# Two 32-key attention stages put in written order, with the norms in quarters and a standing diagonal bank for the causal values

## The chip, the cores and the metric

The kernel runs on one core of one Trainium2 chip. The metric is the device time of one execution in microseconds, as the median of several runs. All data is fp32.

## What is computed

`x` is 64 batches of 32 rows of 256; `ctx_512` is 64 batches of 257 keys of 64. Six blocks follow one another, each adding to `x`:

```python
x = x + L0_xattn(layernorm(x), ctx_512)   # stage A: causal, 16 heads of 16, keys from the context; only its first 32 matter
x = x + L0_attn(layernorm(x))             # stage B: 16 heads of 128, one shared key and value
x = x + L0_ffn(layernorm(x))              # stage C: 4 of 16 blocks chosen per row
x = x + L1_xattn(layernorm(x), ctx_512)   # stage D: 257 rotated keys
x = x + L1_attn(layernorm(x))             # stage E: causal, 16 query heads of 16, 4 key and value groups
x = x + L1_ffn(layernorm(x))              # stage F: one of 8 experts per row
```

The change touches A and E, the two attentions with 32 keys:

```python
# A: no biases; q = x Wq, k, v = ctx Wkv
# E: grouped, with biases
q  = einsum('bse,hed->bhsd', x, Wq) + bq
kg = einsum('bse,ged->bgsd', x, Wk) + bk
vg = einsum('bse,ged->bgsd', x, Wv) + bv
k, v = repeat(kg, 4), repeat(vg, 4)          # over heads
scores = where(causal, einsum('bhqd,bhkd->bhqk', q, k) / sqrt(16), -inf)
out = einsum('bhqk,bhkd->bhqd', softmax(scores), v)
```

## The kernel before

The 2048 rows of `x` are 16 tiles of 128 partitions (`xs[t]`); a tile is four batches. Four tiles are a group (`g`), for which the norm, the transposition and the query and key products are done at once. A loop over tiles does the rest, one slot `t` of the loop working on tile `t + 1` (scores), `t` (the transposed probabilities), `t - 1` (the weighted values), and, in A, `t - 2` (the output product).

A tile's way is: `scores` multiplies queries with keys that stand in a two-wide masked form (`kd`), 32 small matmuls, into four banks of PSUM (tile `S`). `softmax_rows` evicts them with scale and causal mask on VectorE (DVE), takes the row maximum there, subtracts it on GpSimd (POOL), takes exp on ScalarE (ACT), sums on DVE and inverts. In A the division is done on POOL before the transposition, in E after the weighted sum. `heads_on_partitions` transposes the probabilities by TensorE (PE) and copies them out on ACT (`pT`). The values must stand on a block diagonal by head (`vd`), so that one matmul serves four heads: in A four DVE multiplications with the mask `m4` make it from PSUM, in E one DVE addition of the bias (`vb`) and four POOL multiplications. `gather` multiplies.

Layer norms are `ln_group`: statistics of four tiles (`stats`), the inverse root (`rstd_of`; with `power=True` on POOL, an addition and a power), the shift, and four outputs in the tag `xn`, which has four buffers. The normed tiles are transposed into `xT`.

In E, routing for stage F runs beside the attention: `route_stats` a slot after a tile is finished, then for groups of four `route_norm`, `route_turn`, `route` and `send` in successive slots. `send` computes the place of each row and starts one indirect DMA per tile from POOL's queue.

What sets the order: `tc.manual_schedule(engines={PE})` keeps PE in the order of the Python text in A and E; DVE, ACT and POOL are ordered by the planner of the tile framework there. In B all four engines follow the text, in C PE and ACT, in D and F PE. SyncE (SP) issues the plain DMAs in the planner's order everywhere. A scratch area `srt` is filled by SP with 1 MB DMAs, and 12 MB of expert weights (`fw`) load while E begins.

[...] Before, E has S (4), PT, o, and two for the tag "mm", which the transpositions, the query and key products, the value product and the routing products share.

Of the kernel before, what the change touches and what calls it, by code (L numbers as in the profile page):

```python
# [45 lines left out]
def perceiver_kernel(ctx: ExitStack, tc: tile.TileContext, a: dict, out: bass.AP):  # L46
# [107 lines left out]

    def ln_group(g, name, twice=False, act=False, power=False):

        mv = sm(f"lnm_{name}{g}", [P, 4, 2])
        for i in range(4):
            stats(mv[:, i, :], xs[4 * g + i], f"{name}{g}_{i}")
        rs = rstd_of(mv, 4, f"{name}{g}", power)  # L160
        if twice:

            v2 = sm(f"lnw_{name}{g}", [P, 4, 2])
            nc.vector.tensor_tensor(v2[:, :, 1], mv[:, :, 1], rs, ALU.mult)
            nc.vector.tensor_tensor(v2[:, :, 1], v2[:, :, 1], rs, ALU.mult)
            rs2 = rstd_of(v2, 4, f"{name}{g}b", power)
            nc.vector.tensor_tensor(rs2, rs2, rs, ALU.mult)
            rs = rs2
        sh = sm(f"lnh_{name}{g}", [P, 4])
        nc.vector.scalar_tensor_tensor(sh, mv[:, :, 0], -1.0, rs, ALU.mult, ALU.mult)  # L170
        xn = []
        for i in range(4):
            y = xnp.tile([P, D], F32, tag="xn", name=f"xn_{name}{g}_{i}")
            x_ = xs[4 * g + i]
            if act:
                nc.scalar.activation(
                    y, x_, AF.Identity, scale=rs[:, i : i + 1], bias=sh[:, i : i + 1]
                )
            else:
                nc.vector.scalar_tensor_tensor(  # L180
                    y,
                    x_,
                    rs[:, i : i + 1],
                    sh[:, i : i + 1].to_broadcast([P, D]),
                    ALU.mult,
                    ALU.add,
                )
            xn.append(y)
        return xn
# [22 lines left out]
    def softmax_rows(s_ps, t, work, name):  # L212


        s = work.tile([P, NH, S], F32, tag="s", name=f"s_{name}{t}")
        nc.vector.scalar_tensor_tensor(
            s.rearrange("p (r h) k -> p r (h k)", r=4),
            s_ps[:, :, :P],
            0.25,
            bc(caus4, 1, 4),  # L220
            ALU.mult,
            ALU.add,
        )
        mx = sm(f"mx_{name}{t}", [P, NH])
        nc.vector.tensor_reduce(mx, s, AX.X, ALU.max)
        nc.gpsimd.tensor_tensor(s, s, bc(mx, 2, S), ALU.subtract)
        nc.scalar.activation(s, s, AF.Exp)
        su = sm(f"su_{name}{t}", [P, NH])
        nc.vector.tensor_reduce(su, s, AX.X, ALU.add)
        ri = sm(f"ri_{name}{t}", [P, NH])  # L230
        nc.vector.reciprocal(ri, su)
        return s, ri
# [31 lines left out]
    def scores(ps, qT, kd, i, name):  # L264

        s_ps = ps.tile([P, 4, 512], F32, tag="S", name=f"S_{name}")
        for o in range(KC):
            for j in range(4):
                for r in range(4):
                    rs = slice(32 * r, 32 * r + 32)  # L270
                    nc.tensor.matmul(
                        s_ps[j * S : (j + 1) * S, r, o * 64 : (o + 1) * 64],
                        qT[rs, o, i * P + j * S : i * P + (j + 1) * S],
                        kd[rs, o, 4 * i + j].rearrange("p w k -> p (w k)"),
                        start=True,
                        stop=True,
                        tile_position=(32 * r, 32 * j),
                    )
        return s_ps
# [56 lines left out]
    with tc.tile_pool(name="wA", bufs=2) as work, tc.tile_pool(  # L336
# [3 lines left out]
    ) as ps2, tc.manual_schedule(engines={mybir.EngineType.PE}):  # L340
# [15 lines left out]
        def group(g, part):  # L356
# [7 lines left out]
            if part == 0:  # L364
                feats[g][2] = transposed(ln_group(g, "a", power=True), ps2, g, "a")
# [27 lines left out]
        def score(t):  # L393
            g, i = divmod(t, 4)
            qT, kd, _ = feats[g]
            s_ps = scores(ps1, qT, kd, i, f"a{t}")
            sc[t] = softmax_rows(s_ps, t, work, "a")
            s, ri = sc[t]
            nc.gpsimd.tensor_tensor(s, s, bc(ri, 2, S), ALU.mult)
# [56 lines left out]
        for _ in range(18):  # L456
            nc.tensor.matmul(warm, pad[:, 0:P], pad[:, 0:256], start=True, stop=True)
        for part in (0, 1, 2):
            group(0, part)
        score(0)  # L460
        values(0)

# [7 lines left out]
        for t in range(NT + 2):  # L470
# [8 lines left out]
            if t < NT:  # L479
                turned[t] = heads_on_partitions(sc.pop(t)[0], ps1, t, work, "a")  # L480
            if 1 <= t <= NT:
                gather(t - 1)
            group(t // 4 + 1, t % 4)
# [653 lines left out]
    with mbw, wd1:  # L1137
# [3 lines left out]
        with tc.tile_pool(name="wD", bufs=2) as work, tc.tile_pool(  # L1141
# [7 lines left out]

            def e_group_start(g):  # L1150
                feats[g] = (
                    e_w.tile([P, KC, 512], F32, tag="qT", name=f"qTe{g}"),
                    e_w.tile([P, KC, 16, 2, S], F32, tag="kd", name=f"kde{g}"),
# [3 lines left out]
            def e_features(g, part, o, ps):  # L1157

                qT, kd, xT = feats[g]
                q_ps = ps.tile([P, 512], F32, tag="mm", name=f"qe{g}_{o}_{part}")  # L1160
# [193 lines left out]
            steps[48] = lambda: lat.update(e=ln_group(0, "e", power=True))  # L1354
            steps[50] = lambda: e_group_start(0)
            steps[61] = lambda: lat.update(e1=ln_group(1, "e", power=True))
            for z, b_ in enumerate((51, 55, 56, 58, 59, 60)):
# [112 lines left out]
    with tc.tile_pool(name="wE", bufs=2) as work, tc.tile_pool(  # L1470
        name="psE", bufs=1, space=PSUM
    ) as ps1, tc.tile_pool(name="psE2", bufs=2, space=PSUM) as ps2, tc.manual_schedule(
        engines={mybir.EngineType.PE}
    ):
        sc, vals, turned = {}, {}, {}
        lat[1] = lat["e1"]

        def group(g, part):

            if g >= NG:  # L1480
                return
            if part == 0:
                e_group_start(g)
                for k in range(KC):
                    transposed_part(lat.pop(g) if k else lat[g], feats[g][2], ps2, k, f"e{g}")
            if part in (1, 2):
                for o in range(KC):
                    e_features(g, part, o, ps2)
            if part == 3 and g + 1 < NG:
                lat[g + 1] = ln_group(g + 1, "e", power=True)  # L1490

        def score(t):
            g, i = divmod(t, 4)
            qT, kd, xT = feats[g]
            s_ps = scores(ps1, qT, kd, i, f"e{t}")
            sc[t] = softmax_rows(s_ps, t, work, "e")
            v_ps = ps2.tile([P, 4, DC], F32, tag="mm", name=f"ve{t}")
            for j in range(4):
                for k in range(KC):
                    for r in range(4):  # L1500
                        nc.tensor.matmul(
                            v_ps[32 * r : 32 * r + 32, j, :],
                            xT[:, k, i * P + j * S : i * P + (j + 1) * S],
# [4 lines left out]
            vb = work.tile([P, 4, DC], F32, tag="vb", name=f"vbe{t}", bufs=1)  # L1508
            nc.vector.tensor_tensor(vb, v_ps, bc(vec[:, V_BV : V_BV + DC], 1, 4), ALU.add)
            vd = vals[t] = work.tile([P, 4, 4, 4, NH], F32, tag="vd", name=f"vde{t}", bufs=3)  # L1510
            for j in range(4):
                nc.gpsimd.tensor_tensor(
                    vd[:, j],
                    bc(vb[:, j, :].rearrange("p (g d) -> p g d", g=4), 2, 4),
                    bc(bc(m4, 2, 16), 1, 4),
                    ALU.mult,
                )

        def gather(t):
            pT, vd, ri = turned.pop(t), vals.pop(t), sc.pop(t)[1]  # L1520
            o_ps = ps1.tile([P, D], F32, tag="o", name=f"oe{t}")
            for c in range(4):
                for j in range(4):
                    nc.tensor.matmul(
                        o_ps[j * S : (j + 1) * S, c * 64 : (c + 1) * 64],
                        pT[:, c, j * S : (j + 1) * S],
                        vd[:, j, c].rearrange("p h d -> p (h d)"),
                        start=True,
                        stop=True,
                    )  # L1530
            on = work.tile([P, D], F32, tag="on", name=f"one{t}", bufs=1)
            nc.vector.tensor_tensor(
                on.rearrange("p (h d) -> p h d", h=NH),
                o_ps.rearrange("p (h d) -> p h d", h=NH),
                bc(ri, 2, 16),
                ALU.mult,
# [6 lines left out]
        def route_stats(t):  # L1543
            rows[t] = sm(f"lnm_f{t}", [P, 1, 2])
            stats(rows[t][:, 0, :], xs[t], f"f{t}")

        def route_norm(ts):
            n_ = len(ts)
            mv = sm(f"lnq_f{ts[0]}", [P, n_, 2])
            for i, t in enumerate(ts):  # L1550
                nc.gpsimd.tensor_copy(mv[:, i, :], rows[t][:, 0, :])
            rs = rstd_of(mv, n_, f"f{ts[0]}", True)
            sh = sm(f"lnh_f{ts[0]}", [P, n_])
            nc.vector.scalar_tensor_tensor(sh, mv[:, :, 0], -1.0, rs, ALU.mult, ALU.mult)
            rows[ts] = []
            for i, t in enumerate(ts):
                y = xnp.tile([P, D], F32, tag="xn", name=f"xn_f{t}")
                nc.scalar.activation(
                    y, xs[t], AF.Identity, scale=rs[:, i : i + 1], bias=sh[:, i : i + 1]
                )  # L1560
                rows[ts].append(y)
                nc.gpsimd.tensor_copy(xf[t][:, D + 2 : D + 3], rs[:, i : i + 1])
                nc.gpsimd.tensor_copy(xf[t][:, D + 3 : DP], sh[:, i : i + 1])
# [115 lines left out]

        score(0)  # L1680
        group(1, 0)
        group(1, 1)
        for t in range(NT + 1):


            if t + 1 < NT:
                score(t + 1)
            if t < NT:
                turned[t] = heads_on_partitions(sc[t][0], ps1, t, work, "e")
            if t > 1:  # L1690
                group(t // 4 + 1, t % 4)
            if t > 0:
                gather(t - 1)
                route_stats(t - 1)
            for step, ts in routing.get(t, ()):
                step(ts)
        for step, ts in routing[NT + 1]:
# [192 lines left out]
```

## Time and profile before

| | us |
|---|---|
| median of 3 runs | 1302.73 (1302.47 to 1304.62) |
| the profiled execution | 1298.15, of which its span 1296.4 |
| A: first scores to the last `ya` | 18.5 to 151.5 |
| B, C and D | 151.5 to 992.5 |
| E: first scores to the last `oe` | 992.5 to 1125.3 |
| routing's end, to the first row fetched | 1125.3 to 1146.9 |
| F | 1146.9 to 1296.4 |

The stages are cut by the timeline of PE. Busy time of PE is modelled and includes time at a lower clock, so a busy PE is not PE at its peak. A group's row names the line, the engine, the operation, output and input, count, busy time, mean time of one, and the idle time before it with what ended most of that. "issue" is a wait for nothing that the profile shows.

### The profile page before, as it was taken

What the parts mean: (1) busy time and instruction counts of PE and PEld (TensorE: products, weight loads), DVE (VectorE), ACT (ScalarE), POOL (GpSimd) and SP (SyncE); (2) the same over time, 40 slices, a digit from 0 to 9 for tenths busy, and PEclk for the clock granted to TensorE, in tenths of its full rate; (3) what the DMA queues carried; (4) which work ended last, traced back from release to release, by engine and by line L of the source; (5) the groups of instructions that cost most, each with busy time, mean ns of one, the idle gap of its engine ahead of it and who ended that gap; (6) DMA issues with size and microseconds to landing.
All of it is one profiled execution on the core that took longest, in us unless ns stands there. A gap on an engine that the chain in (4) does not pass through costs nothing. (4 is left out here: it accounts for less than half of the span.)

```text
span 1296.4 us, 26028 instructions
## 1 busy us (share of the span) xinstructions
PE 1187.8 (92%) x10189; PEld 833.3 (64%) x10189; DVE 769.0 (59%) x1751; ACT 540.1 (42%) x1255; POOL 389.7 (30%) x504
## 2 busy tenths in 40 slices
PE   6898999999999999999989999999998687669997
PEld 4555767767767566777756767777766455536664
DVE  5665345778758865533288877777674574334432
ACT  2336354554544641222365656556563233211111
POOL 2232251554524631000055252000002577621111
PEclk8889999999999989979999989999999788669999
DMA  7991110111021220912154353111103700011110
GB/s 232 309 332 36 28 42 1 41 42 41 25 83 42 59 65 2 283 33 68 44 149 131 62 143 93 46 35 48 34 1 127 266 3 19 22 50 42 43 39 18
DMA packets 94588, 103.10 MB, mean 80 GB/s; under 512 B 37664, under 2 KB 71201, under 8 KB 93986
## 3 DMA queue, kind: packets, MB, share of 16 engines
q1 hardware_dynamic: 92594, 97.19, 25.8%
q0 software_dynamic: 1872, 4.23, 0.9%
q8 instruction: 82, 1.34, 0.4%
q14 instruction: 40, 0.33, 0.1%
HBM read 69.45 MB, written 32.85 MB: 79 GB/s over the span
## 5 line engine op out<-in xcount | busy, mean ns | idle before, releaser
L1261 ACT ACTIVATE pp<-Sd,nm 128x257 f32<-128x257 f32 x256 | 118.2, 475 | 71.9 <-DVE nm L1257 66.1
L706 PE MATMUL qb<-xT_b,b_q 128*128 128x256 f32 x512 | 123.0, 389 | 0.0
L706 PEld LDWEIGHTS qb<-xT_b,b_q 128*128 128x128 f32 x512 | 95.6, 191 | 39.5 <-issue 19.6
L797 PE MATMUL yb<-b_o,oTb 128*128 128x256 f32 x512 | 116.1, 386 | 0.0
L797 PEld LDWEIGHTS yb<-b_o,oTb 128*128 128x128 f32 x512 | 98.4, 194 | 14.3 <-issue 1.0
L1270 DVE TENSOR_TENSOR pp<-pp,rd 128x514 f32<-128x514 f32 x128 | 98.4, 769 | 2.1
L1257 DVE TENSOR_REDUCE nm<-Sd 128x2 f32<-128x514 f32 x128 | 83.0, 685 | 19.2 <-PE Sd L1249 19.0
L1292 ACT COPY pTd<-pt 128x512 f32<-128x512 f32 x112 | 61.5, 599 | 52.1 <-PE pt L1286 52.1
L1309 PE MATMUL od<-pTd,na 128*64 128x256 f32 x480 | 66.3, 397 | 8.2 <-issue 6.5
L725 POOL TENSOR_TENSOR q2b<-qTb 128x512 f32<-128x512 f32 x64 | 65.2, 1048 | 27.0 <-ACT qTb L714 27.0
L1249 PE MATMUL Sd<-ct,qTd 64*128 64x257 f32 x480 | 69.2, 405 | 0.4 <-ACT pp L1261 0.2
L816 POOL TENSOR_TENSOR ynb<-ynb,vec 128x256 f32<-128x256 f32 x16 | 11.6, 726 | 191.3 <-DVE ynb L815 191.3
L714 ACT COPY qTb<-qb 128x512 f32<-128x512 f32 x64 | 37.5, 585 | 72.2 <-PE qb L706 70.6
L1286 PE MATMUL pt<-cst,pp 128*128 128x128 f32 x512 | 66.9, 274 | 0.0
L1286 PEld LDWEIGHTS pt<-cst,pp 128*128 128x128 f32 x512 | 59.0, 141 | 9.9 <-issue 5.6
L1068 PE MATMUL qd<-xT_d,d_m 128*128 128x256 f32 x256 | 64.4, 395 | 0.2 <-ACT xT_d L201 0.2
L759 DVE RECIPROCAL rqb<-rqb 128x512 f32<-128x512 f32 x16 | 53.5, 3344 | 17.8 <-ACT rqb L754 17.8
L588 PE MATMUL yc<-c,hc 128*128 128x256 f32 x256 | 59.4, 388 | 2.7 <-DVE hc L583 2.7
L1325 PE MATMUL yd<-d_n,co 128*128 128x256 f32 x256 | 61.5, 395 | 0.0
L1765 POOL DMA_INDIRECT out_dram<-os,ti x23 | 22.7, 986 | 124.4 <-DVE os L1762 100.8
L1068 PEld LDWEIGHTS qd<-xT_d,d_m 128*128 128x128 f32 x256 | 46.8, 192 | 17.0 <-issue 6.4
L773 DVE RECIPROCAL rdb<-denb 128x512 f32<-128x512 f32 x16 | 53.7, 3355 | 5.8 <-PE denb L771 5.6
(365 smaller groups left out, 2394.5 us busy)
## 6 DMA issues: line engine op xcount, KB each, us to landing
srt<-pad SPq DMA_DIRECT2D x17, 1040.0 KB
mb<-maskd SPq DMA_DIRECT2D x64, 128.0 KB
ct<-ctd SPq DMA_DIRECT2D x30, 257.0 KB
rct<-in_ctxT_dram SPq DMA_DIRECT2D x32, 128.5 KB
rrt<-in_ctxT_dram SPq DMA_DIRECT2D x64, 64.2 KB
ctd<-rct SPq DMA_DIRECT2D x32, 128.5 KB
nad<-rna SPq DMA_DIRECT2D x16, 256.0 KB
fw<-in_f_wg_dram SPq DMA_DIRECT2D x8, 512.0 KB
```

Source lines behind the costliest of these rows:

```text
L706: nc.tensor.matmul(q_ps[:, hh, :], b_q[:, k, h * P : (h + 1) * P], xT[:, k, c0 : c0 + 256], start=(k == 0), stop=(k == KC - 1),)
L725: nc.gpsimd.tensor_tensor(q2[:, 4 * h4 : 4 * h4 + 4, :], q, q, ALU.mult)
L797: nc.tensor.matmul(y_ps, oT[:, h, :], b_o[:, h, :], start=(h == 0), stop=(h == NH - 1))
L1068: nc.tensor.matmul(q_ps[:, r, :], m[:, k, pr * P : (pr + 1) * P], xT[:, k, c0 : c0 + 256], start=(k == 0), stop=(k == KC - 1),)
L1249: nc.tensor.matmul(s_ps[:, hh, :NKV], qT[hs, b % 8, 4 * u : 4 * u + 4, :], ct[hs, b % 4, :], start=True, stop=True,)
L1257: nc.vector.tensor_reduce(nm, s_ps[:, :, :NKV], AX.X, ALU.max, negate=True)
L1261: nc.scalar.activation(pp[:, hh, :], s_ps[:, hh, :NKV], AF.Exp, bias=nm[:, hh : hh + 1], accum_out=sd[:, hh : hh + 1],)
L1270: nc.vector.tensor_tensor(pp, pp, bc(rd, 2, NKV), ALU.mult)
L1286: nc.tensor.transpose(pt[:, hh * 256 + u * P : hh * 256 + u * P + P], probs[b][:, u, hh, c * P : (c + 1) * P], ident,)
L1292: nc.scalar.copy(pT[:, c, :], pt)
L1309: nc.tensor.matmul(o_ps[64 * hh : 64 * hh + 64, 0, :], na[:, j, c, :], pT[:, c, hh * 256 : (hh + 1) * 256], start=(c == 0), stop=(c == 1),)
L1325: nc.tensor.matmul(y_ps, co[:, pr, :], n[:, pr, :], start=(pr == 0), stop=False)
```

## The change

- A: DVE, ACT and POOL follow the text as PE does; E: DVE and ACT do, POOL stays with the planner.
- `ln_group` is split into `ln_scale` and `ln_out`, and `norm` does a group's norm in four quarters, one in each slot, two groups ahead. The first two groups are still normed at once, ahead of the loop.
- A: exp (`power`) and the row sums with the division (`share`) get places of their own in the slot. The key product is done in a group's first slot, then transpositions, then queries.
- E: the row sums fall away. Three standing `vd` tiles, filled with zeros and with ones in a 17th column of their diagonal blocks, take the values by four copies of 32 partitions each, one on DVE and three on ACT; the weighted sum gives the row sum in column 17. They are set up on POOL in stage D.
- E: the value bias is added to `xs` on POOL after the norm has read it, since the probabilities of a row sum to one. The key product is done for one half only, as both halves of the heads use the same keys; `kd` has half the size.
- E: the value product has its own PSUM bank "v", and "mm" has one bank in place of two.
- E: `route_norm` takes statistics of a group from one tile, and its small copies on POOL become fewer.

The diff, cut to its core:

```diff
+    def norm(g, part, name, mvs, lat):
+        if g >= NG:
+            return
+        two = range(2 * (part % 2), 2 * (part % 2) + 2)
+        if part == 0:
+            mvs[g], lat[g] = sm(f"lnm_{name}{g}", [P, 4, 2]), []
+        if part < 2:
+            for i in two:
+                stats(mvs[g][:, i, :], xs[4 * g + i], f"{name}{g}_{i}")
+        else:
+            lat[g] += [ln_out(xs[4 * g + i], *mvs[g], i, f"{name}{g}") for i in two]
+        if part == 1:
+            mvs[g] = ln_scale(mvs[g], f"{name}{g}", power=True)
...
-                        kd[rs, o, 4 * i + j].rearrange("p w k -> p (w k)"),
+                        kd[rs, o % kd.shape[1], 4 * i + j].rearrange("p w k -> p (w k)"),
...
-    ) as ps2, tc.manual_schedule(engines={mybir.EngineType.PE}):
+    ) as ps2, tc.manual_schedule(
+        engines={
+            mybir.EngineType.PE,
+            mybir.EngineType.DVE,
+            mybir.EngineType.Activation,
+            mybir.EngineType.Pool,
+        }
+    ):
...
-                feats[g][2] = transposed(ln_group(g, "a", power=True), ps2, g, "a")
+                feats[g][2] = transposed(lat.pop(g), ps2, g, "a")
...
+        def power(t):
+            nc.scalar.activation(sc[t], sc[t], AF.Exp)
+
+        def share(t):
+            s = sc[t]
+            su = sm(f"su_a{t}", [P, NH])
+            nc.vector.tensor_reduce(su, s, AX.X, ALU.add)
+            ri = sm(f"ri_a{t}", [P, NH])
+            nc.vector.reciprocal(ri, su)
             nc.gpsimd.tensor_tensor(s, s, bc(ri, 2, S), ALU.mult)
...
+        lat, mvs = {0: ln_group(0, "a", power=True)}, {}
         for part in (0, 1, 2):
             group(0, part)
         score(0)
         values(0)
+        power(0)
+        share(0)
+        lat[1] = ln_group(1, "a", power=True)
...
-                turned[t] = heads_on_partitions(sc.pop(t)[0], ps1, t, work, "a")
+                turned[t] = heads_on_partitions(sc.pop(t), ps1, t, work, "a")
+            if t + 1 < NT:
+                power(t + 1)
             if 1 <= t <= NT:
                 gather(t - 1)
-            group(t // 4 + 1, t % 4)
+            group(t // 4 + 1, (2, 0, 1, 3)[t % 4])
+            norm(t // 4 + 2, t % 4, "a", mvs, lat)
+            if t + 1 < NT:
+                share(t + 1)
             for step in first.get(t, ()):
                 step()
...
+            vd = [
+                e_w.tile([P, 4, 4, 4, NH + 1], F32, name=f"vde{z}", bufs=1) for z in range(3)
+            ]
+            def e_values():
+                for vd_ in vd:
+                    nc.gpsimd.memset(vd_, 0.0)
+                    nc.gpsimd.tensor_copy(
+                        vd_.rearrange("p j c h d -> p (j c) h d")[:, :, :, NH], bc(m4, 1, 16)
+                    )
+            def e_bias(t):
+                x4 = xs[t].rearrange("p (c h d) -> p c h d", c=4, h=4)
+                bv = vec[:, V_BV : V_BV + DC].rearrange("p (c d) -> p c d", c=4)
+                nc.gpsimd.tensor_tensor(x4, x4, bc(bv, 2, 4), ALU.add)
...
             steps[48] = lambda: lat.update(e=ln_group(0, "e", power=True))
+            steps[49] = lambda: [e_bias(t) for t in range(4)]
+            steps[53] = e_values
             steps[50] = lambda: e_group_start(0)
             steps[61] = lambda: lat.update(e1=ln_group(1, "e", power=True))
-            for z, b_ in enumerate((51, 55, 56, 58, 59, 60)):
+            steps[62] = lambda: [e_bias(t) for t in range(4, 8)]
+            for z, b_ in enumerate((51, 55, 56, 58, 59)):
...
-    ) as ps1, tc.tile_pool(name="psE2", bufs=2, space=PSUM) as ps2, tc.manual_schedule(
-        engines={mybir.EngineType.PE}
+    ) as ps1, tc.tile_pool(name="psE2", bufs=1, space=PSUM) as ps2, tc.manual_schedule(
+        engines={
+            mybir.EngineType.PE,
+            mybir.EngineType.DVE,
+            mybir.EngineType.Activation,
+        }
...
+        def place_values(t, v_ps):
+            for r in range(4):
+                rs = slice(32 * r, 32 * r + 32)
+                dst = vd[t % 3][rs].rearrange("p j c h d -> p (j c) h d")[:, :, r, :NH]
+                src = v_ps[rs].rearrange("p j (c d) -> p (j c) d", c=4)
+                if r == 0:
+                    nc.vector.tensor_copy(dst, src)
+                else:
+                    nc.scalar.copy(dst, src)
...
+            ri = sm(f"ri_e{t}", [P, NH])
+            nc.vector.reciprocal(ri, o_ps[:, :, NH])
...
+        v_ps = {}
         score(0)
-        group(1, 0)
-        group(1, 1)
+        v_ps[0] = values(0)
+        power(0)
+        for fn in group(1, 0) + group(1, 1):
+            fn()
+        place_values(0, v_ps.pop(0))
         for t in range(NT + 1):
+            parts = group(t // 4 + 1, t % 4) if t > 1 else []
             if t + 1 < NT:
                 score(t + 1)
-            if t < NT:
-                turned[t] = heads_on_partitions(sc[t][0], ps1, t, work, "e")
-            if t > 1:
-                group(t // 4 + 1, t % 4)
+            for fn in parts[:1]:
+                fn()
             if t > 0:
                 gather(t - 1)
-                route_stats(t - 1)
+            for fn in parts[1:]:
+                fn()
+            if t + 1 < NT:
+                v_ps[t + 1] = values(t + 1)
+            if t + 1 < NT:
+                power(t + 1)
+            if t < NT:
+                turned[t] = heads_on_partitions(sc.pop(t), ps1, t, work, "e")
+            if t + 1 < NT:
+                place_values(t + 1, v_ps.pop(t + 1))
+            if t >= NT - 1:
+                route_stats(t - 1)
             for step, ts in routing.get(t, ()):
                 step(ts)
+            norm(t // 4 + 2, t % 4, "e", mvs, lat)
+            if t % 4 in (0, 3) and 0 < (t + 1) // 4 < NG - 1:
+                bias((t + 1) // 4 + 1, t % 4 == 0)
+            if 0 < t < NT - 1:
+                route_stats(t - 1)
```

## The prediction

> **What bounds the kernel now.** I read the page first, then a table of windows by stage, then the timelines, waits and groups inside the two stages that the diff touches.
>
> ```profile
> PE 1187.8 (92%) x10189; PEld 833.3 (64%) x10189; DVE 769.0 (59%) x1751; ACT 540.1 (42%) x1255; POOL 389.7 (30%) x504
> PE   6898999999999999999989999999998687669997
> PEclk8889999999999989979999989999999788669999
> ```
>
> TensorE is the fullest engine, but its row dips, and the granted clock dips with it, at the start (the first 32-key attention, "stage A") and in slices 31 to 36 (the second, "stage E"). The windows, whose columns are length, busy time of PE, weight load, DVE, ACT and POOL, granted clock, DMA share and GB/s:
>
> ```profile
> 18.50:151.50 133.00, 111.02 (x2274) 70.96 (x2275) 80.66 (x208) 52.74 (x103) 38.97 (x41) 0.90 0.63 198
> 151.50:992.50 841.00, 811.89 (x4541) 585.86 (x4539) 547.56 (x1148) 411.15 (x1011) 224.38 (x224) 0.98 0.23 63
> 992.50:1125.30 132.80, 101.83 (x2776) 73.43 (x2776) 70.26 (x194) 43.85 (x77) 88.06 (x180) 0.82 0.29 106
> 1125.30:1146.90 21.60, 9.53 (x42) 8.06 (x38) 10.11 (x59) 3.93 (x10) 13.14 (x31) 0.50 0.14 50
> ```
>
> The 841 us between are PE at a clock of 0.98; nothing much is to be had there. In A and E no engine is full: they lose time to waits between engines, and then to the clock. Stage A's timeline of DVE shows one cause:
>
> ```profile
> 20.70 0.74 DVE L152 BATCH_NORM_STATS2 lnb_a<-x 128x6 f32<-128x256 f32 x2
> ...
> 26.43 0.16 DVE L170 SCALAR_TENSOR_TENSOR lnh_a<-lnm_a,lnr_a 128x4 f32<-128x4 f32 x1 [1.47 <-POOL lnr_a L140]
> 26.51 0.68 DVE L216 SCALAR_TENSOR_TENSOR s_a<-S_a,caus 128x512 f32<-128x512 f32 x1
> ```
>
> The first scores are ready at 20.0, but the planner's order has DVE norm later groups until 26.5, and PE stands 6.1 us. In E, waits and PE's timeline:
>
> ```profile
> DVE su_e L229 <- ACT s_e L227: 23.2, 10, 6.2
> PE ve L1501 <- issue: 6.5, 3, 3.0
> 1064.31 1.11 PE L209 MATMUL tp_e<-cst,xn_e 128*128 128x128 f32 x4 [3.06 <-DVE vbe L1509]
> 1068.59 0.64 PE L1616 MATMUL rank<-cum,one 128*128 128x32 f32 x2 [1.58 <-DVE cum L1605]
> 1117.14 0.66 PE L1571 MATMUL tpf<-cst,xn_f 128*128 128x128 f32 x4 [2.76 <-DVE vbe L1509]
> ```
>
> DVE sits before the row sums until exp is done, and what it does late (`vbe`, which frees the "mm" bank; `cum`) stops PE.
>
> **What the skill says.** (1) The Trainium skill, "TensorE: Matmul & The Clock Gate", section "What's actually happening": about 3.4 us of idleness halve the clock. The trace agrees: after the 6.1 us wait the clock is 0.50 from 25 to 30 us. So a wait costs more than its length. (2) "Runtime: NRT & Kernel Launch", section "Instruction fetch mechanics": instructions arrive in blocks of 256, "mostly hidden". Here not: PE's waits for "issue" of 3.02 and 2.50 us, at 1004.7 and 1011.3, are exactly 128 matmuls and 128 weight loads apart, while the 12 MB of expert weights load. The edit cannot remove those. (3) The first of these pages, section "Architectural detail: the array is 16× 32×32, not 1× 128×128": ScalarE and VectorE queues are strict FIFO. So under a written order one late instruction holds all behind it; the trace shows nothing against it.
>
> **Stage A, part by part.** The arithmetic stays; the order changes. PE at full clock needs for a tile S 0.8, ya 1.06, va 1.03, ptp 0.6, oa 1.1 = 4.6 us, and for a group (four tiles) transposes 1.4, queries 3.6, keys 1.95 = 6.9; so 25.3 per group. Measured, S of tile 3 (43.3) to S of tile 15 (136.5): 93.2/3 = 31.1.
> - Key product first, queries last: S no longer waits behind four kda evictions of 0.6 (1.2 us per group) but behind one qTa eviction (about 0.5).
> - vda before the row sums: va's two mm banks come free about 1 us earlier (now 0.4 to 1.0 us before tp or qa).
> - In quarters, DVE's statistics are 1.2 us a tile; in the second quarter DVE also waits for POOL's power (0.23 + 1.04 + handoff): 1.7 us, which delays the next scores' eviction by some 0.8.
> On POOL that power now stands between a tile's subtraction and its division; POOL is 29% busy here, so only DVE waits. No DMA is moved.
> So 26.6 per group: (26.6 − 31.1) × 3 = −13.4. At the start ln_group(1) moves behind share(0), but still ahead of tile 1's eviction; walking the queues gives S of tile 3 at 40.4, not 43.3: −2.9. Against it, keys_norm(0) at slot 9 is now one block in DVE's queue: statistics 4 × 0.61, twice POOL 1.27 + 0.3, four small operations 0.7 = 6.2, of which about 1.6 is slack; tile 11's eviction and vda, and through their banks PE, wait: +4.6. Sum −11.7. SP still pushes 10 fills of 1 MB from 45 us, and the clock is 0.69 to 0.84 there; I give back 2.7 for dips that stay: **−9**.
> The trace shows keys_norm(1), which belongs to the next stage, running at 104 and 122 us, inside A. If the stricter order pushes it past A, its statistics 2.4, a table load 1.28 and eight small steps stand before qTb's copies: +5 at most, 0 at least; I take **+1**.
>
> **Before E.** One key product less for group 0 (four passes of 0.45 at 969.7, PE full): −1.8. The new POOL work (three memsets and copies, no row of their size; 1.0 us each by the 512-wide POOL rows scaled to 1088 would be 2.2; eight bias adds of 0.72) lies where POOL is idle from 836 to 992; it may slow DVE (beside POOL's subtraction, DVE's lnh_e took 1.00 us at 1056.8 in place of 0.16), so 0 to +1. **−1.5**.
>
> **Stage E.** Removed per tile: vde on POOL 4 × 0.59, vbe 0.41 on DVE, the row sums 0.68; per group one key product (1.8 PE, 1.5 ACT). Added per tile: a 32x256 copy on DVE (nearest row vbe 0.41) and three on ACT (nearest row oTa's 0.37 each; bound 0.3 to 0.45): +1.1 on ACT. POOL goes from 6.6 to 4.7 us a tile, DVE from 5.7 to 5.0, ACT from 3.4 to 4.2, PE to 6.0, against the 8.3 (132.8/16) that a tile takes. So none is full; the queues decide.
> What goes wrong is the one mm bank (two before) and ACT's order: evictions, exp, pT, three placements, routing. Walking the four kinds of slot, with DMA issues on POOL 4 × 1.27: slot 3 (route) is PE-bound, 5.0; slot 0 (transposes, send) 5.5; slot 1 (queries, route_norm): the first query's eviction waits behind the placement, which waits for exp, which waits for a DVE late by 4 after route's chain: 8.8; slot 2 (keys, route_turn): DVE is late by 5 (two waits for POOL's power in slot 1), so exp ends 8.7 into the slot, and the second transposition waits for an eviction behind exp, pT and placement: 11.7. Sum 31.0 per group.
> Measured S of tile 4, 8, 12 at 1021.8, 1053.5, 1088.7, last oe ending 1125.3: 31.7, 35.2, 36.6. After: 27.5 (no route, no send at first), 31.0, 29 (no group parts): −16.0. Up to tile 4, the ACT order makes the start slower (S of tile 1 at +11.4, not +8.0), and the lighter slots after it win it back; the fetch waits stay: −0.5. POOL's order is still the planner's; waits of 4 to 5 us in slots 1 and 2 cost half-clock windows, +5 over the stage. **−11.5**.
> The tail (1125 to 1147) is a chain of small steps at half clock plus POOL's eight DMA issues; the merged copies save 1: **−1**. The last stage (149.5 us) is untouched.
>
> **Sum.** −9 + 1 − 1.5 − 11.5 − 1 = −22. The profiled execution took 1298.15 (span 1296.4 and 1.75 around it); the median of the runs is 1302.73, 4.6 more, all in one narrow band, so I apply −22 to the median: 1281.
>
> **Rivals.** (a) *PE becomes the bound* in both stages: E at 6.0 a tile, say 97 + 6 for fetch instead of 133, A −12, rest −3.5: −46, 1257. For it: no engine sum exceeds PE's. Against: in E the written order chains POOL's power to DVE to ACT to the one mm bank. Chance 0.26.
> (b) *The one mm bank is the new wait*: every hand-over in E (nine per group and five at the start, 32 in all) waits for an ACT queue that waits for POOL. I counted about 1 us apiece; PE waits of 2.8 and 3.1 us for a bank freed late stand in the trace with two banks. From 0.7 us more each the gain of 22 is gone; at 1 us more: 1281 + 32 = 1313. Against: before, the evictions came late by the planner's order, not by need. Chance 0.20.
> (c) *The order is not the planner's fault*: DMA and fetch set the pace, nothing moves by over 0.2%: 0.04, 1302. It is a real possibility only if gains and losses cancel.
> Forecast: 0.50. The range takes in both ends of the unknown costs and most of (a) and (b): 1256 to 1307. Faster by over 0.2% (2.6 us, about what a measurement here tells from none): 0.50 + 0.26 = 0.76; within: 0.04; slower: 0.20.
>
> **What would show it.** Right: tile 0's eviction at about 20 us and PE's 6.1 us wait gone; S_a about 26.6 us per group; one DVE stretch of 6 us near slot 9 with PE idle behind it; no vde multiplications; S_e about 31 us per group with PE idle before tpf and qe for ACT evictions. Wrong: S_e groups under 26 (rival a) or over 35 (rival b), keys_norm(1) after A's last ya, or a change in the 841 us between.

## The result, and the profile after

The changed kernel is slower: 1309.49 us as the median of 20 runs (1302.69 to 1317.01), against 1300.72 for the kernel before on the same chip; the ratio is 1.0066, 95% interval 1.0040 to 1.0091. The forecast was −22 us. The profiled execution took 1308.71 us, 1306.9 of it span. From its page, the rows that answer to those of before:

```profile
PE 1194.0 (91%) x10173; PEld 838.7 (64%) x10173; DVE 764.2 (58%) x1740; ACT 553.9 (42%) x1295; POOL 364.6 (28%) x430
PE   7998999999999998999989999999998688669997
PEclk8799899999999989979989989999999888669999
```

POOL has become lighter, as the diff says, and PE has 16 matmul records fewer; the two dips in PE's row stand where they stood. The windows by stage of the same trace (length; busy PE, weight load, DVE, ACT, POOL; clock; DMA share; GB/s):

```profile
19.34:153.74 134.40, 115.00 (x2273) 75.08 (x2274) 80.83 (x216) 52.82 (x103) 39.89 (x42) 0.86 0.62 193
153.74:1005.92 852.18, 816.07 (x4537) 588.53 (x4536) 552.61 (x1148) 409.78 (x1009) 235.23 (x239) 0.97 0.23 62
1005.92:1135.60 129.68, 98.11 (x2764) 71.19 (x2764) 61.20 (x180) 58.94 (x119) 54.14 (x98) 0.82 0.31 108
1135.60:1161.20 25.60, 10.25 (x39) 8.34 (x39) 12.21 (x63) 3.94 (x10) 11.25 (x23) 0.53 0.15 50
```

A gained nothing (133.0 to 134.4), E gained 3 of the 11.5 us forecast, and 11 us were lost in the 841 between, where the forecast named a change as a sign that it was wrong. The last row ends at F's first product and not at the first row fetched; on that cut the kernel before has 24.2 us there.

One profiled execution is not enough to book that loss. The same instructions take different times: in this study's profiles C, which no kernel here touches, takes 131.5 us at a clock of 0.95 or up to 138.2 at 0.91. Stage lengths in us, from PE's timeline (the tail up to F's first product):

| profiled execution | A | B | C | D | E | tail |
|---|---|---|---|---|---|---|
| before | 133.0 | 360.0 | 132.8 | 348.4 | 132.7 | 24.2 |
| after | 134.4 | 359.8 | 134.6 | 357.8 | 129.7 | 25.6 |
| after, a second time | 140.4 | 360.0 | 138.2 | 355.5 | 129.7 | 25.3 |
| A's edit alone | 136.9 | 360.0 | 138.1 | 353.0 | 133.1 | 24.5 |
| E's edit alone | 143.5 | 356.9 | 135.2 | 356.6 | 130.6 | 25.3 |
| the repaired kernel (`fw_late`, below) | 122.6 | 359.8 | 131.6 | 351.1 | 115.2 | 22.6 |

So I read times from repeated runs, and from the traces which waits stand where. Single waits repeat well: 5.62 us before `ka` and 1.49 us in D stand in both profiles of the changed kernel. Sums of waits do not: in these two profiles PE's waits for "issue" in A add up to 10.2 and 13.9 us, and its waits for ACT in E to 15.7 and 20.4.

### The profile page after: what moved, and what is told of

Same layout as the page of the kernel before. It is cut to its first block, busy times and chain, and to the rows that moved or that the text cites. A ratio compares the mean times of both kernels' runs of the same rounds, so it can differ in the third digit from the quotient of the medians.

```text
span 1306.9 us, 25963 instructions
## 1 busy us (share of the span) xinstructions
PE 1194.0 (91%) x10173; PEld 838.7 (64%) x10173; DVE 764.2 (58%) x1740; ACT 553.9 (42%) x1295; POOL 364.6 (28%) x430
## 5 line engine op out<-in xcount | busy, mean ns | idle before, releaser
L1331 DVE TENSOR_TENSOR pp<-pp,rd 128x514 f32<-128x514 f32 x128 | 102.0, 797 | 2.1
L1370 PE MATMUL od<-pTd,na 128*64 128x256 f32 x480 | 67.7, 404 | 12.3 <-issue 10.9
L1386 PE MATMUL yd<-d_n,co 128*128 128x256 f32 x256 | 64.7, 410 | 0.0
L1386 PEld LDWEIGHTS yd<-d_n,co 128*128 128x128 f32 x256 | 51.1, 205 | 14.2 <-issue 6.9
L628 PEld LDWEIGHTS yc<-c,hc 128*128 128x128 f32 x256 | 50.1, 198 | 12.5 <-DVE hc L623 3.5
```

Of the source, the lines that this page charges most:

```text
L628: nc.tensor.matmul(y_ps, hs[f][:, i * P : (i + 1) * P], c_2[:, f, :], start=(f == 0), stop=(f == 7),)
L1331: nc.vector.tensor_tensor(pp, pp, bc(rd, 2, NKV), ALU.mult)
L1370: nc.tensor.matmul(o_ps[64 * hh : 64 * hh + 64, 0, :], na[:, j, c, :], pT[:, c, hh * 256 : (hh + 1) * 256], start=(c == 0), stop=(c == 1),)
L1386: nc.tensor.matmul(y_ps, co[:, pr, :], n[:, pr, :], start=(pr == 0), stop=False)
```

## The experiments

**The two halves alone.** `a_only` is the changed kernel with E and its preparation in D as before, `e_only` the same with A as before.

> The edit of stage A alone; stage E and what it sets up in D are as before. Theory 1 (the trace of after: A 1.5 us longer because waits for "issue" take back what the order gained, B and C 2 us longer, D's 9 us belong to what E put into D): 0 to +4 us against before, D as long as before. Rival (D became longer because the edit of A shifted its transfers and POOL's rotation against PE): +7 to +11 us, D about 9 us longer than before with none of E's bias additions in it.

> The edit of stage E and of its preparation in D alone; stage A is as before. Theory 1: +5 to +8 us against before (D +9, E -3, tail +1), the bias additions of POOL visible as PE's waits of about 1.5 us in D at two places. Rival (D's loss comes through A): -4 to 0, D as long as before.

Measured: A alone 1.0018 (0.9996 to 1.0039; 1307.4 against 1303.0), E alone 1.0013 (0.9989 to 1.0038; 1304.8). The rival falls: D's new waits come with E's part (below), not through A, though D took 353.0 us in the one profile of `a_only`, and not the 348.4 of before. But E alone cost less than theory 1 said, and the halves sum to some 4 us, not 8.6; with 3 us of uncertainty on each half, that difference is at the edge of what these runs can tell.

**The bias in D.** The eight additions of `e_bias` for tiles 0 to 7 leave D and stand behind the weighted sums of those tiles in E:

```diff
-            steps[49] = lambda: [e_bias(t) for t in range(4)]
-            steps[62] = lambda: [e_bias(t) for t in range(4, 8)]
...
             nc.gpsimd.tensor_tensor(xs[t], xs[t], on, ALU.add)
+            if t < 8:
+                e_bias(t)
```

> The changed kernel, with the value bias of tiles 0 to 7 added on POOL in stage E, behind each tile's weighted sum, in place of D. Theory 1 (the additions in D slow DVE's copies beside POOL, and PE waits for them): -3 us against after, PE's two waits of 1.49 us in D gone. Rival (D's loss lies elsewhere, in its transfers): within 1 us of after, or up to 3 us slower through POOL's longer queue in E.

Measured: 1.0018 (0.9995 to 1.0041), where the changed kernel has 1.0066 and, measured again below, 1.0073: 6 to 7 us less, give or take 4. The timeline of the changed kernel in D, then that of `bias_late`:

```profile
876.11 1.12 POOL L1206 TENSOR_TENSOR x<-x,vec 128x256 f32<-128x256 f32 x1 [27.91 <-DVE xn_e L178]
876.55 0.95 DVE L178 SCALAR_TENSOR_TENSOR xn_e<-x,lnr_e,lnh_e 128x256 f32<-128x256 f32 x1
...
877.50 1.28 DVE L1318 TENSOR_REDUCE nm<-Sd 128x2 f32<-128x514 f32 x2
877.58 0.73 POOL L1206 TENSOR_TENSOR x<-x,vec 128x256 f32<-128x256 f32 x1 [0.36 <-DVE plast L1333]
...
880.34 1.12 POOL L1206 TENSOR_TENSOR x<-x,vec 128x256 f32<-128x256 f32 x1 [0.36 <-DVE xn_e L178]
...
880.98 1.03 DVE L1331 TENSOR_TENSOR pp<-pp,rd 128x514 f32<-128x514 f32 x1
882.12 0.68 DVE L1355 COPY pTd<-pt 128x512 f32<-128x512 f32 x1
883.10 1.08 PE L1370 MATMUL od<-pTd,na 128*64 128x256 f32 x8 [1.49 <-issue]
```

```profile
878.50 0.48 DVE L178 SCALAR_TENSOR_TENSOR xn_e<-x,lnr_e,lnh_e 128x256 f32<-128x256 f32 x1
...
878.97 1.29 DVE L1318 TENSOR_REDUCE nm<-Sd 128x2 f32<-128x514 f32 x2
...
882.14 0.69 DVE L1331 TENSOR_TENSOR pp<-pp,rd 128x514 f32<-128x514 f32 x1
883.94 0.44 PE L1370 MATMUL od<-pTd,na 128*64 128x256 f32 x2 [0.37 <-issue]
```

Beside POOL's addition DVE's `xn_e` takes 0.95 in place of 0.48 and `pp` 1.03 in place of 0.69, so the copy `pTd` is late and PE, which starts `od` 0.3 us after its end, stands 1.49 us (labelled "issue"). The wait of 1.48 to 1.50 us stands at both places in all five profiles that have the bias in D, and is 0.37 to 0.39 in all twelve that have not. The Trainium skill, "SBUF — State Buffer", section "Who interferes with whom", says that a DVE instruction with two SBUF inputs contends with a GpSimd instruction that reads SBUF, and that the second to issue blocks. The trace agrees: both DVE operations have two SBUF inputs, while the pair of reductions `nm`, whose one input is in PSUM, takes 1.28 us beside a POOL addition and 1.29 without one. The two waits themselves are worth 2.2 us, less than the runs show; the rest is not located. Part of it may lie in E: of the kernels with E's edit and one "mm" bank, E took 129.7 to 133.9 us in the five profiles with the bias in D and 125.4 to 128.2 in the three without. Why is not shown.

**The fills.** The scratch area's 17 DMAs of 1 MB read a copy of the pad that DVE makes only when A's last sum is done, so they run in B; first on the changed kernel, then on the kernel before.

```diff
+        padz = const.tile([P, DP], F32, name="padz")
+        nc.vector.tensor_copy(padz[:, D:DP], pad[:, D:DP])
+        nc.vector.tensor_scalar_mul(padz[:, 0:D], xs[NT - 1], 0.0)
...
-  srt[r0 : r0 + NE * P].rearrange("(j p) c -> p j c", p=P), bc(pad, 1, NE)
+  srt[r0 : r0 + NE * P].rearrange("(j p) c -> p j c", p=P), bc(padz, 1, NE)
```

> The changed kernel, with the 17 fills of the scratch area held back until stage A's last sum (they read a copy of the pad that DVE makes then). Theory 1 (transfers of 17 MB beside A make the instruction fetch late): PE's waits for "issue" of 10 us in A go, A is 8 to 12 us shorter than in after, and the time is 1298 to 1302. Rival (the fetch waits do not depend on the transfers, or they move into B): A as long as in after, time within 2 us of after.

> The kernel before, with the 17 fills of the scratch area held back until stage A's last sum, as in the run with this edit on the changed kernel. Theory 1 (in the old order PE waits for engines long enough for the instruction fetch to finish behind those waits, so the transfers cost it little): -3 to +1 us against before, PE's waits for engines in A about 20 us as before. Rival (the fills cost both orders alike, by fetch or by something else): -7 to -10 us, as they brought the changed kernel.

Measured: on the changed kernel 0.9985 (0.9967 to 1.0004), 10 to 11 us less than without; on the kernel before 0.9990 (0.9965 to 1.0015), nothing that can be told. PE's waits in A, of the changed kernel and then of `fills_b` (total us, times, longest):

```profile
PE ka L399 <- issue: 5.6, 1, 5.6
PE S_a L285 <- issue: 2.7, 2, 2.0
PE oa L466 <- issue: 1.9, 1, 1.9
```

```profile
PE oa L466 <- DVE x L483: 6.3, 2, 4.5
PE ka L399 <- issue: 5.6, 1, 5.6
```

The waits for "issue" before `S_a` and `oa` go with the fills. The second stands 253 matmuls and 259 weight loads after the first, the third 383 and 385 after the second: exactly two and three times 256 instructions. The prediction cited blocks of 256 instructions, so this fits instruction fetch. The trace of the changed kernel also holds the transfers of instructions, one row of its page (packets, MB, share of the DMA engines' time):

```profile
q8 instruction: 81, 1.33, 0.4%
```

These are 81 packets of 16 KB for PE's 20,346 matmuls and weight loads. A packet takes about 1 us, with the fills beside it or not. What differs is when it starts. PE crosses a boundary of 256 instructions seven times between 53 and 101 us. There the packet starts 3.4 us (median) after the crossing in the changed kernel and 0.2 us before it in `fills_b`. In the kernel before it starts 2.9 us after, and with the fills held back 0.6 us before. So the fetch is late in both orders, by about as much. In the old order PE waited for other things at the same time: 20.7 us in A, 2.4 of them put down to its own earlier products, with 1.2 for "issue", and taking the fills away from it brings nothing that can be told. So theory 1 holds on both kernels: part of what the new order won was time in which the fetch had been hidden. The three waits are 4.6 of the 10 to 11 us (8.3 in the second profile); the rest is not located.

But the largest wait, 5.6 us before `ka`, stays. It lies 474 matmuls and 482 weight loads before the next, no multiple of 256, and no packet of that queue starts between 28.8 and 41.9 us. Theory 1 had counted it as fetch.

**The block of key norms, and the wait before `ka`.** `combo1` takes `fills_b` and `bias_late` and splits `keys_norm(0)` over three slots; `combo2` also loads the weights of B and C in pieces, each held by a small DVE write in its slot.

```diff
-            9: [lambda: keys_norm(0)],
+            8: [lambda: keys_part(0)],
+            9: [lambda: keys_part(1)],
+            10: [lambda: keys_part(2)],
```

> The changed kernel with fills held back, with the value bias of tiles 0 to 7 added in E, and with keys_norm(0) in three parts in slots 8, 9 and 10 (two tiles' statistics each, then scale and outputs) in place of one block in slot 9. Theory 1: against the run with the fills alone A loses PE's waits of 4.5 and 1.8 us for the output sum (x), D about 4 us: 1290 to 1293, 9 to 12 us under before. Rival (waits only move to other places): 1297 to 1301.

> The same, and the weights of B and C (6.4 MB, which load from 13 to 45 us) paced: b_kv in slot 3, b_q in four pieces in slots 4 to 7, b_o in four pieces in slots 8 to 11, c_1 and c_2 after A. Theory 1 (PE's 5.6 us of "issue" before the key product of group 1 is an instruction fetch slowed by these transfers): that wait falls under 1.5 us, A 3 to 5 us shorter, and the clock of 0.54 from 30 to 40 us goes: 1286 to 1290. Rival (that fetch is slow whatever is transferred): the wait stays between 5 and 6 us, time as in the run before it.

`combo1`: 0.9926 (0.9895 to 0.9957), some 8 us under `fills_b`, near the 10 that theory 1 gave the split and the bias together (1294.68 us, where it said 1290 to 1293). How much of that is the split cannot be told, since the bias alone brought 6 to 7. The block was real: its larger wait, 4.5 us in `fills_b`, shrinks to 1.45, while one of 1.8 us for a later `x` stays. Timelines of the changed kernel and of `combo1`, the product that waits for the bank of tag "o", which DVE's late addition to `x` frees:

```profile
109.13 1.66 PE L466 MATMUL oa<-pT_a,vda 128*64 128x32 f32 x32 [3.97 <-DVE x L483]
```

```profile
106.78 1.13 PE L466 MATMUL oa<-pT_a,vda 128*64 128x32 f32 x32 [1.45 <-DVE x L483]
```

`combo2`: 0.9902 (0.9886 to 0.9918), not told apart from `combo1`, and the wait before `ka` is still 5.16 us with a DMA share of 0.08 and then 0.02 beside it (windows of `combo2`):

```profile
25.00:30.00 5.00, 1.12 (x4) 0.72 (x4) 3.41 (x10) 0.59 (x1) 1.43 (x3) 0.50 0.08 15
30.00:35.00 5.00, 3.52 (x4) 1.16 (x4) 3.84 (x11) 1.90 (x3) 1.93 (x2) 0.50 0.02 3
```

My theory of that wait falls. The timeline of the changed kernel, all engines, shows another:

```profile
25.20 0.37 DVE L152 BATCH_NORM_STATS2 lnb_a<-x 128x6 f32<-128x256 f32 x1
...
29.05 1.67 DVE L178 SCALAR_TENSOR_TENSOR xn_a<-x,lnr_a,lnh_a 128x256 f32<-128x256 f32 x4
...
31.96 1.41 DVE L451 TENSOR_TENSOR vda<-va,cst 128x256 f32<-128x256 f32 x4
...
32.81 1.19 PE L399 MATMUL ka<-ctxa,a_kv 64*128 64x512 f32 x1 [5.62 <-issue]
```

`ka` starts 0.85 us into the four `vda` copies of tile 1, that is just after the second of them ends, at 32.71, and frees their "mm" bank; and DVE reaches them late because the norm of group 1 is written ahead of them. "issue" here is a wait for a bank that the profile did not attribute. `ln1` tests it: the changed kernel with that norm moved to where DVE is idle.

```diff
+        lat[1] = ln_group(1, "a", power=True)
         score(0)
         values(0)
         power(0)
         share(0)
-        lat[1] = ln_group(1, "a", power=True)
```

> The changed kernel with the norm of group 1 in A written ahead of the first scores, where DVE stands idle from 9 to 19 us, in place of behind the first division. Theory 1, as the last runs changed it (PE's 5.6 us before the key product at 32.8 are no instruction fetch, since they stay with the transfers taken away: the bank of that product comes free only when DVE, which has the norm of group 1 written ahead of tile 1's evictions, has copied tile 1's values): the wait falls under 1 us, the clock of 0.5 from 30 to 40 us goes, A 4 to 8 us shorter than in after, time 1302 to 1306. Rival (a slow fetch at that point of the program, whatever DVE does): the wait stays above 4 us, time as after.

The wait is gone (timeline of `ln1`):

```profile
26.24 1.41 DVE L451 TENSOR_TENSOR vda<-va,cst 128x256 f32<-128x256 f32 x4
...
27.08 1.95 PE L399 MATMUL ka<-ctxa,a_kv 64*128 64x512 f32 x4
```

A takes 126.8 us, 7.6 less than in the first profile of the changed kernel: 5.6 for the wait, and the clock of 0.50 that stood from 30 to 40 us is 1.00. That second part does not always come with the first: in `combo4` and `a_fix` below the wait is gone too, and the clock from 30 to 40 us is still 0.53 and 0.50. The run as a whole: 1.0024 (1.0001 to 1.0047), about 6 us less than the changed kernel, give or take 4, its median (1306.46) just above what was expected. So the wait for the bank is shown.

**E's banks and its loads.** `combo3` is `combo1` with the value product in two "mm" banks; `combo4` is `combo3` with `ln1`'s move.

```diff
-name="psE2", bufs=1, space=PSUM
+name="psE2", bufs=2, space=PSUM
...
-            v_ps = ps1.tile([P, 4, DC], F32, tag="v", name=f"ve{t}")
+            v_ps = ps2.tile([P, 4, DC], F32, tag="mm", name=f"ve{t}")
```

> The run with fills, bias and keys_norm changed, and in E the value product in the tag "mm" with two banks, in place of one bank of its own beside one "mm" bank. Theory 1 (the one mm bank costs E: waits of tpf, tp_e and qe for ACT evictions add up to some 14 us): those waits fall under 5 us, E 5 to 8 us shorter. Rival (the hand-over is bound by ACT's order, not by banks; or the value product, held until its placement, now takes the bank that others need): E within 2 us, or up to 4 us longer.

> The run with fills held back, the bias in E, keys_norm in three parts and two "mm" banks in E, and with the norm of group 1 ahead of the first scores. Theory 1: against that run without the last edit 4 to 8 us less, 1278 to 1282, A at 117 to 120. Rival (the gain comes back as a lower clock later on): A shorter, the time within 2 us of the run without.

`combo3`: 0.9890 (0.9862 to 0.9917), its interval over that of `combo1`. PE's waits in E for the two kernels, the changed one (one bank) and `combo3`:

```profile
PE tpf L1654 <- ACT xTf L1657: 6.9, 3, 2.7
...
PE tp_e L229 <- ACT xT_e L230: 3.3, 2, 2.8
```

```profile
PE tpf L1669 <- ACT vde L1611: 5.6, 3, 2.1
...
PE tp_e L229 <- ACT xT_e L230: 2.8, 1, 2.8
```

The waits changed their name more than their size: with two banks `tpf` waits for the placement that holds the other bank, on the same ACT queue. All of E's waits for ACT went from 15.8 us (`combo1`) to 12.8, not under 5; over all profiles of E's edit they are 15.4 to 20.4 with one bank and 12.8 to 17.6 with two. So most of them stay, as the rival said. But E was 4.4 us shorter (127.7 to 123.3), where the rival allowed 2, and the tail 2.2 us shorter. The bank has a share, and ACT's order holds the larger part of the waits. `combo4`: 0.9829 (0.9778 to 0.9880), A 119.6.

`combo5` and `fw_late` treat the 12 MB of expert weights: paced, two loads in each of slots 0 to 11, or held back altogether until slots 8 to 15, by a DVE write ahead of each load (in `combo5`, of each after slot 0's).

> The same, and the 24 loads of expert weights (12 MB, at once at E's start) paced, two in each of E's first twelve slots. Theory 1 (PE's waits for "issue" in E, some 9 us, lie 128 matmuls apart and are instruction fetches slowed by these loads): they fall under 3 us, E 5 to 8 us shorter than in the run before it. Rival (the fetch is slow in E for another reason, as GpSimd's own transfers): they stay above 7 us.

> The repaired kernel with E's expert weights (12 MB) held back until E's slots 8 to 15. Theory 1 (the fetch waits in E's first eight slots come from these loads, and pacing them over twelve slots was not thin enough): no wait for "issue" over 1 us before slot 8, new ones may come after it. Rival (the fetch is slow there for another reason): waits for "issue" of 2 to 4 us stay in slots 1 to 5 with next to no transfer beside them.

`combo5`: 0.9802 (0.9752 to 0.9852), E's waits for "issue" still 8.2 us; pacing did not remove them. `fw_late`: 0.9757 (0.9713 to 0.9800), 1269.38 against 1300.93 us, the fastest kernel of this study by its median, though its interval overlaps those of `combo4` and `combo5`. A window near E's start of `combo4`, whose loads all run there, then two of `fw_late`, near E's start and later:

```profile
1010.00:1030.00 20.00, 16.33 (x520) 11.62 (x515) 12.51 (x30) 8.91 (x18) 10.12 (x13) 0.78 0.76 266
```

```profile
1000.00:1020.00 20.00, 17.02 (x650) 11.80 (x639) 15.87 (x40) 12.56 (x26) 14.74 (x20) 1.00 0.02 5
...
1062.00:1083.00 21.00, 14.99 (x561) 13.15 (x561) 10.95 (x44) 6.58 (x15) 8.14 (x13) 0.83 0.65 214
```

With next to no transfers beside E's first eight slots, two waits for "issue" are left in them, 0.64 and 0.96 us, where `combo4` has 2.12, 3.48 and 0.18; the clock is 1.00 up to 1020 us and 0.91 from there to 1040. One wait of 2.58 us comes at 1083, where the loads now run, 14 times 256 instructions after the last. The packets of instructions agree: at the three boundaries ahead of these waits they start 3.2 to 3.8 us after the crossing in the changed kernel and in `combo4`, and 0.1 to 0.5 us after it in `fw_late`. So these waits do come from the loads. The Trainium skill's "mostly hidden" ("Runtime: NRT & Kernel Launch", "Instruction fetch mechanics") does not hold here for a dense run of small matmuls beside bulk transfers; without them it nearly does.

**The whole and the repaired parts.** `after_again` is the changed kernel; `a_fix` A's edit with its three repairs (norm of group 1, key norms, fills) and E as before; `e_fix` E's edit with bias and banks repaired and A as before.

> The changed kernel once more, unaltered. Theory 1 (the whole is its parts: A about 0, D +4.6 by the bias, E -2, tail +1, and no more): +2 to +5 us against before. Rival (the two parts cost more together than alone, by the clock): +7 to +11 us again.

> The edit of A alone, E and D as before, with its three repairs: norm of group 1 ahead of the first scores, keys_norm in three parts, fills held back. Theory 1: A at 118 to 121 against 133 to 143 before, -12 to -17 us against before. Rival (the clock of B, C and D takes it back): A as short, the time only -5 us or less.

> The edit of E alone, A as before, with its two repairs: the bias added in E, and two "mm" banks. Theory 1: E at 120 to 124 against 131 to 133, D as before, -7 to -11 us against before. Rival (E's gain in the last runs came from A's repairs, through a cooler start): -3 us or less.

Measured: 1.0073 (1.0052 to 1.0094), 0.9901 (0.9864 to 0.9937), 0.9948 (0.9923 to 0.9972). The loss repeats, at the size that the rival gave; that the clock causes it is not shown. `a_fix` is −0.99%, some −13 us, with A at 123.0 in its profile; `e_fix` −0.52%, −6.8, E 124.7. The first fits theory 1 in time, with A 2 us longer than it said; the second lies just outside it, in time and in E.

## Why the prediction was wrong, by its own steps

- **A −9: wrong; measured about nothing.** The per-group step (26.6 us) was near: with `a_fix` S of tile 3 to S of tile 15 takes (121.66 − 39.4)/3 = 27.4, in the changed kernel 30.4 (32.1 in its second profile). Two terms failed. At the start I saw the norm of group 1 ahead of tile 1's eviction and still put S of tile 3 at 40.4; it came at 43.06, as before (43.26). The 6.1 us wait was not removed; it went from the scores to the key product, whose bank the same DVE queue holds. The key norms' block was sound: +4.6 forecast, a wait of 4.0 measured, 1.45 after the split. And I held fetch fixed ("the edit cannot remove those"), without asking what it hid behind: 1.2 us of waits for "issue" in A became 4.6 of fetch (8.3 in the second profile), besides the 5.6 mislabelled. The fills were also misread: there are 17 in A, not 10, and the clock in 10 us windows beside them is 0.69 to 0.99, not 0.69 to 0.84.
- **A to B, +1: not seen.** B takes the same time before and after; the key norms of group 1 stay inside A.
- **D −1.5: wrong sign.** The bias was bounded at 0 to +1. The row that I used (`lnh_e` at 1.00 beside POOL) showed the mechanism; I priced it by POOL being idle, not by which DVE operation feeds PE there. `bias_late` puts the bias at 6 to 7 us, of which 2.2 are located.
- **E −11.5: 3.0 measured.** PE's waits for DVE in E fell from 12.3 to 5.7, those for ACT rose from 9.5 to 15.7 (20.4 in the second profile): a change of releaser. The hand-overs through ACT were mis-sized, at about 1 us apiece. This is rival (b)'s mechanism in milder form, and, as the two banks show, more ACT's order than the bank, though the bank has a share. The groups took 30.6, 34.0 and 34.4, not 27.5, 31.0 and 29. The slow start was right in kind (S of tile 1 at +13.5, forecast +11.4).
- **Tail −1: +1.4 in the first profile (24.2 to 25.6).** In the kernels with two banks it is 22.5 to 23.1.
- **The likeliest case at 0.50, and 0.20 for slower.** At 1309 us the result lies between the likeliest case and rival (b)'s 1313, but E, where (b) put the loss, came out 3 us shorter: the number is near (b)'s by other causes. The holes in A and E have one form: a wait was struck out without asking what else ended at the same moment. Behind a DVE wait stood a bank, a fetch, or ACT.

What stays open: the located waits are less than the runs' differences, 2.2 of 6 to 7 us for the bias and 4.6 to 8.3 of 10 to 11 for the fills. A's and E's parts alone cost some 4 us, together 9, a difference at the edge of the noise. In the repeated runs of the kernel before and of the changed one, 0.001 of mean granted clock goes with 0.5 to 1.6 us, and the mean clock is 0.940 before, 0.937 with either part, and 0.933 with both. At an equal clock of 0.936 straight-line fits give 1306.7 us for the changed kernel and, on four chips, 1304.3 to 1307.1 for the kernel before, so most of the loss goes with the clock. That says in which form the loss comes, not what starts it: from 30 to 40 us the clock is 0.50 in the changed kernel, behind the wait at `ka`, 1.00 in `ln1`, and 0.50 again in `a_fix`, where PE has no wait over 0.4 us in that time.

## What to carry to other kernels

When a written order removes a wait, look for the next user of the same engine's queue (here the bank behind `vda`) and for what was hidden in the wait, instruction fetch first; give bulk loads a place where a late fetch does not show (B took 359.8 us with the fills and without). A cheap operation on an idle engine is priced by what it does to the engine that shares its port, at the place where PE depends on that engine. And compare stages by waits that repeat, not by the lengths of one profiled execution.

## What was not expected of the hardware

- The label "issue" covered three things: fetch delays, which follow the transfers (4.1 to 8.3 us of waits in A in five profiles of the new order with the fills, at most 1.6 in eight without), a plain wait for a PSUM bank (5.6 us), and one for a DVE copy (1.49).
- Beside bulk transfers an instruction packet does not take longer, about 1 us, but starts some 3 us later, in the old order as in the new.
- The same 17 MB of transfers cost the new order 10 to 11 us, give or take 3, and the old one nothing that can be told (1.3 us, give or take 3.3).
- DVE at 0.95 in place of 0.48 us, and POOL at 1.12 in place of 0.73, when both read SBUF.
- An untouched stage of 131.5 us varies by 6.7 us with the granted clock.
